# Local attention layers: a cell's attention in one piece instead of two halves, and a new order of the cell's steps

## The chip, the core and the metric

The kernel runs on one core of a Trainium2 chip. The core has five engines with queues of their own, each of which takes its instructions strictly in the order written: PE (TensorE: matrix products and transposes), DVE (VectorE), ACT (ScalarE: activations and copies), POOL (GpSimd) and SP (SyncE, which here issues every DMA). They meet only at semaphores. The metric is the time of one execution on the device in microseconds; the runs of a kernel are summed up by their median. The kernel before took 2453.49 us (median of three runs, 2446.65 to 2457.55).

## The reference

The program has two stages. The first (AdaLN, a 16-head attention, a mixture of experts, a linear-memory attention) is not touched by the change. The second is a stack of six local-attention layers, each followed by a gated feed-forward part, on four sequences (B) of 512 tokens with 128 channels:

```python
def attn_layer(x, Wqkv, qs, ksc, Wo):
    q, k, v = jnp.split(x @ Wqkv, 3, -1)          # 16 heads of 64
    q = l2norm(q) * qs
    k = l2norm(k) * ksc
    q = q * cos * scale + rotate_half(q) * sin * scale
    k = k * cos * inv + rotate_half(k) * sin * inv
    out = local_attention(q, k, v)                # windows of 32, each sees 64 keys
    return out @ Wo
...
for i in range(DEPTH):                            # 6 layers
    x = attn_layer(shift_tokens(x), ...) + x
    x = ffn_layer(shift_tokens(x), ...) + x
```

`local_attention` forms scores of 32 queries with 64 keys, masks them, takes a softmax over the 64 and multiplies with the values. `shift_tokens` moves half of the channels by one token.

## The kernel before

**Cells.** The work of the six layers is cut into 96 cells, numbered n: layer l, sequence b, group j of four heads (j = 0 to 3, the fastest). A cell's work is spread over four passes of one loop (`for n in range(-4, NC + 1)`). While cell n is in its attention, cell n+1 has its rotated queries and keys scaled and regrouped, cell n+2 gets its norms and values, and cell n+3 (`nx`) its projections.

**Steps and engines**, by line of the kernel before:

- `project(nx, w)`: two products into the PSUM tile `pq` (one buffer of two banks), w = 0 for queries, 1 for keys (L831).
- `rotate(nx, w)`: two DVE passes over `pq` (L841, L842), then two on POOL (L843, L844).
- `square(nx, w)`: ACT squares `pq` (L849). `pq` is free for the next projection after both.
- `norms(n+2)`: products into the bank `nb` (L859), a DVE clamp into `rn` (L868), Ln and Exp on ACT (L870, L872, each with a table load ahead of it), four DMAs into `rb` (L878). It calls `place("N")`, `place("L")`, `place("X")` between them.
- `scale(n+1)`: POOL multiplies keys and queries by `rb` (L886). `gather(n+1, w)`: four DMAs each into `kd` (keys) and `qd` (queries) (L899).
- `values(n+2)`: products into two banks (L910), each copied by ACT (L917), and three DMAs (L919 to L921).
- `scores(n, u)`: for half u of the windows, two mask products (L934), 64 small products (L940), DVE maximum and subtraction (L949, L951). `exponential` on ACT (L960), `normalise` on DVE (L965 to L967).
- `turn(n, u)`: four transposes (L974), a copy by ACT (L976). `weigh(n, u)`: 64 products with the values (L989), two copies (L1001).
- `output(n-1)`, in cells with even j: eight PE passes (L1009), added to `zT` by DVE (L1010).

**Feed-forward.** After the fourth group of a sequence `feed` runs as a coroutine: `place(name)` lets it go on where it has stopped at that name. Its stops are, in order: Z (two DMAs that shift `zT` into `xsf`, L809 and L810), D (mean `lm`, L1037; subtraction L1039; square L1041), N (variance `lv`, L1044), L (Ln, L1046), X (Exp, L1048), A (normalised input `xn`, L1051 and L1052), B (two hidden products `phf`, L1022), G (gelu, L1027), B (two more), G, C (gate, L1031), A (two more with gates), B (result `pyf`, L1072). It spans four cells: Z and D fall into the cell with j = 0, N to G into j = 1, B and G into j = 2, C, A, B into j = 3.

**What sets the order.** Nothing reorders: each engine's queue is the order in which the loop calls the steps. The pool `ps_g` holds two banks for `nb`, the values, `output` and all products of `feed`.

Of the kernel before, what the change touches and what calls it, by code (L numbers as in the profile page):

```python
# [46 lines left out]
def adaln_kernel(ctx: ExitStack, tc: tile.TileContext, a: dict):  # L47
# [368 lines left out]
    class First:  # L416
# [41 lines left out]
        def settle(self):  # L458
            pass
# [307 lines left out]
    with ExitStack() as ph:  # L767
# [83 lines left out]
        def norms(n):  # L851

            d = live[n]
            nb = bank("nb", (P, S // 2))
            for h in range(2):
                for w in range(2):
                    for x in range(2):
                        c = 32 * (2 * w + x)
                        mm(  # L859
                            nb[c : c + 32, :],  # L860
                            nsel,
                            d["sq", w][:, h, x * (S // 2) : (x + 1) * (S // 2)],
                            start=(h == 0),
                            stop=(h == 1),
                            skip_group_check=True,
                        )
            rn = att.tile([P, S // 2], F32, name="rn")
            vec.tensor_scalar(rn, nb, 1e-24, None, ALU.max)  # L868
            place("N")
            act(rn, rn, AF.Ln, scale=65536.0)  # L870
            place("L")
            act(rn, rn, AF.Exp, scale=-0.5, bias=nsh_t)  # L872
            place("X")
            rb = d["rb"] = work.tile([P, 2, S], F32, name="rb", bufs=1)
            for w in range(2):
                for x in range(2):
                    c = 32 * (2 * w + x)
                    nc.sync.dma_start(  # L878
                        rb[:, w, x * (S // 2) : (x + 1) * (S // 2)],
                        rn[c : c + 32, :].unsqueeze(1).broadcast_to([32, 4, S // 2]),  # L880
                    )
# [6 lines left out]
        def gather(n, w):  # L888

            d = live[n]  # L890
            t = d["k" if w else "q"]
            if w:
                d["k"] = kts[n % 2]
                y = d["k"][:, :, WIN:]
            else:
                y = d["q"] = cel.tile([P, 2, S], F32, name="qd", bufs=2)
            for c in range(2):
                for h in range(2):
                    nc.sync.dma_start(y[h::2, c, :], t[64 * c : 64 * c + 64, h, :])  # L899

        def values(n):


            l, b, j = cells[n]
            c0 = 2 * INNER + j * 4 * HDW
            vo, ve = live[n]["v"] = vos[n % 3], ves[n % 3]
            for y in range(0, TB, 2):
                pv = bank("pv2", (P, 2, 4 * HDW))
                for t in range(2):
                    mm(  # L910
                        pv[:, t, :],
                        shifted[b][:, (y + t) * P : (y + t + 1) * P],
                        layers[l][0][:, c0 : c0 + 4 * HDW],
                        start=True,
                        stop=True,
                    )
                nc.scalar.copy(vo[:, y : y + 2, :], pv)  # L917
                yield
            nc.sync.dma_start(ve[0:64], vo[32:96])  # L919
            nc.sync.dma_start(ve[96:P], vo[0:32])  # L920
            nc.sync.dma_start(ve[64:96, 1:], vo[96:P, 0 : TB - 1])  # L921


        def scores(n, u):
            d = live[n]
            q, k = d["q"], d["k"]


            if u == 0:
                d["s"] = ps_s.tile([P, 2, UW, GK], F32, name="s2")  # L930
            s = d["s"][:, :, 4 * u : 4 * u + 4, :]
            for w in range(2):
                m = wmask_b[:, 1 if u == 0 and w == 1 else 0, 0:4, :]
                mm(s[:, w], ident_b, m, start=True, stop=False, skip_group_check=True)  # L934
            for i in range(4):
                for w in range(2):
                    t0 = (u * UW + 2 * i + (w + i + 1) % 2) * WIN
                    for x in range(4):
                        r, c = slice(64 * (x % 2), 64 * (x % 2) + 64), 32 * ((x + w) % 4)
                        mm(  # L940
# [4 lines left out]
                            stop=True,  # L945
                            skip_group_check=True,
                        )
            nm = att.tile([P, 2, 4], F32, name="nm2")
            vec.reduce_max(nm, s, axis=AX.X)  # L949
            p = d["p", u] = att.tile([P, UW, GK], F32, name="p2")  # L950
            vec.tensor_tensor(  # L951
                p.rearrange("p (i w) k -> p w i k", w=2),
                s,
                nm.unsqueeze(3).broadcast_to([P, 2, 4, GK]),
                ALU.subtract,
            )

        def exponential(n, u):
            p = live[n]["p", u]
            act(p, p, AF.Exp)  # L960

        def normalise(n, u):
            p = live[n]["p", u]
            sm = att.tile([P, UW], F32, name="sm2")
            vec.reduce_sum(sm, p, axis=AX.X)  # L965
            vec.reciprocal(sm, sm)
            vec.tensor_tensor(p, p, sm.unsqueeze(2).broadcast_to([P, UW, GK]), ALU.mult)  # L967

        def turn(n, u):

            p = live[n].pop(("p", u))
            pt = ps_t.tile([P, 4, P], F32, name="pt2", tag="pt2")
            for i in range(4):
                tr(pt[:, i, :], p[:, 2 * i : 2 * i + 2, :].rearrange("p w k -> p (w k)"), ident)  # L974
            pT = live[n]["pT", u] = att.tile([P, 4, P], F32, name="pT2")
            nc.scalar.copy(pT, pt)  # L976

        def weigh(n, u):
            d = live[n]
            pT = d.pop(("pT", u))  # L980

            po = [ps_o.tile([P, 2, 4, WIN], F32, name="po2"), ps_t.tile([P, 2, 4, WIN], F32, name="po2b", tag="pt2")]
            for i in range(4):
                for x in range(4):
                    c = 64 * (x % 2)
                    for w in range(2):
                        r = slice(64 * w, 64 * w + 64)
                        c1 = 32 * ((x + w) % 4)
                        mm(  # L989
                            po[w][c : c + 64, x // 2, i, :],  # L990
                            d["v"][(w + i) % 2][r, 2 * u + i // 2, 64 * x : 64 * x + 64],
                            pT[r, i, c1 : c1 + 32],
                            start=True,
                            stop=True,
                        )
            if u == 0:
                d["o"] = cel.tile([P, 2, 2, S // 2], F32, name="oT2", bufs=2)
            o = d["o"][:, u].rearrange("p h (a w q) -> p (h a) w q", w=4, q=WIN)
            for w in range(2):
                y = po[w].rearrange("p h (a b) q -> p (h a) b q", b=2)  # L1000
                nc.scalar.copy(o[:, :, 0::3, :] if w else o[:, :, 1:3, :], y)  # L1001

        def output(n):
# [76 lines left out]
        def place(name):  # L1080
# [3 lines left out]
            if running and running[1] == name:  # L1084
                try:
                    running[1] = next(running[0])
                except StopIteration:
                    running.clear()
                return True
            return False  # L1090

        turns = [(2, 3, 0, 0), (3, 0, 0, 1), (3, 1, 1, 0), (3, 2, 1, 1)]
        load_rotations(0)
# [2 lines left out]
        for n in range(-4, NC + 1):  # L1096
            nx = n + 3 if 0 <= n + 3 < NC else None
            here = 0 <= n < NC
            if here:
                scores(n, 0)  # L1100
            if 0 <= n + 1 < NC:
                scale(n + 1)
                gather(n + 1, 1)
            if n > 0:
                weigh(n - 1, 1)
            if here:
                exponential(n, 0)
            if 0 <= n + 2 < NC:
                norms(n + 2)
            elif n + 2 >= NC:  # L1110
                for name in "NLX":
                    place(name)
            place("C")
            if 0 <= n + 1 < NC:
                gather(n + 1, 0)
            if nx is not None:
                l, b, j = cells[nx]
                if l + 1 < DEPTH:
                    if (b, j) == (2, 0):
                        layers[l + 1] = load_layer(l + 1)  # L1120
                    if (b, j) == (2, 1):
                        load_rotations(l + 1)
                project(nx, 0)
            if here:
                normalise(n, 0)
            if nx is not None:
                rotate(nx, 0)
            if n > 0 and cells[n - 1][2] % 2 == 1:
                output(n - 1)
            place("Z")  # L1130
            if n + 4 < NC and cells[n + 4][2] == 0:
                b = cells[n + 4][1]
                shifted[b] = shift_in(b, xss[b % 2])
            if here:
                scores(n, 1)


            pieces = values(n + 2) if 0 <= n + 2 < NC else iter(())
            if n % 2:
                next(pieces, None)  # L1140
            if nx is not None:
                square(nx, 0)
            for _ in pieces:
                pass
            if here:
                exponential(n, 1)
            place("A")
            if here:
                turn(n, 0)
                normalise(n, 1)  # L1150
            if nx is not None:
                project(nx, 1)
                rotate(nx, 1)
            if here:
                weigh(n, 0)
            place("B")
            early_square = not place("G") and nx is not None
            if early_square:
                square(nx, 1)
            if here:  # L1160
                turn(n, 1)
            if nx is not None:
                if not early_square:
                    square(nx, 1)
                l, b, j = cells[nx]
                for b1, j1, w, h in turns:
                    if (b1, j1) == (b, j) and l + 1 < DEPTH:
# [109 lines left out]
```

## Time and profile before

| | us |
|---|---|
| median of three runs | 2453.49 |
| the profiled execution | 2440.67 |
| its span | 2438.9 |
| first mask product of the layers (L934) | 686.4 |
| first mask product of the last cell | 2388.2 |
| PE busy | 2164.8 (89%) |
| DVE / ACT / POOL busy | 1573.1 / 1400.7 / 1069.5 |

The layers thus take from about 686 us to the end. The 95 distances between the first mask products of neighbouring cells sum to 1701.8 us, 17.9 us a cell. In a layer's first two sequences the usual distances are 16.9 (j = 0), 16.2 (1), 18.0 (2) and 18.8 us (3), 69.9 us for a round of four. In the last two, when the next layer's weights and tables are loaded, single cells take 20 to 27 us. A page of the profile gives busy time by engine, the granted PE clock in 40 slices, and groups of instructions; a busy PE includes the time in which a product drains while the next is already running.

### The profile page before, as it was taken

What the parts mean: (1) busy time and instruction counts of PE and PEld (TensorE: products, weight loads), DVE (VectorE), ACT (ScalarE), POOL (GpSimd) and SP (SyncE); (2) the same over time, 40 slices, a digit from 0 to 9 for tenths busy, and PEclk for the clock granted to TensorE, in tenths of its full rate; (3) what the DMA queues carried; (4) which work ended last, traced back from release to release, by engine and by line L of the source; (5) the groups of instructions that cost most, each with busy time, mean ns of one, the idle gap of its engine ahead of it and who ended that gap; (6) DMA issues with size and microseconds to landing.
All of it is one profiled execution on the core that took longest, in us unless ns stands there. A gap on an engine that the chain in (4) does not pass through costs nothing.

```text
span 2438.9 us, 76498 instructions
## 1 busy us (share of the span) xinstructions
PE 2164.8 (89%) x33628; PEld 1233.3 (51%) x33628; DVE 1573.1 (65%) x2258; ACT 1400.7 (57%) x2211; POOL 1069.5 (44%) x690
## 2 busy tenths in 40 slices
PE   6889999887678998998899998999899998999996
PEld 3345454443245555555555555555555555555553
DVE  3344544443267677777677777777777777777873
ACT  1334334533356576666676766667666666676662
POOL 1000101010365475555755566555665556555550
PEclk9989999998799899999999999999999999999997
DMA  2200000000156745566555755557555665555550
GB/s 75 65 2 1 3 1 2 1 1 1 47 128 144 182 105 135 123 164 160 126 119 132 197 129 123 124 135 192 128 121 128 157 170 123 122 129 130 137 134 24
DMA packets 164760, 251.23 MB, mean 103 GB/s; under 512 B 28742, under 2 KB 90380, under 8 KB 163404
## 3 DMA queue, kind: packets, MB, share of 16 engines
q1 hardware_dynamic: 164428, 246.34, 41.7%
q8 instruction: 264, 4.33, 0.8%
q14 instruction: 68, 0.56, 0.1%
HBM read 34.27 MB, written 1.05 MB: 14 GB/s over the span
## 4 chain that ended last, share of the span: by engine, by line
PE 52%; DVE 11%; ACT 11%; issue 10%; SPq 5%; DMA 5%; POOL 5%; POOLq 0%; DVEq 0%; ACTq 0%
PE pq L831 7%; PE po L989 5%; PE py L1009 4%; PE s L286 4%; PE pv L910 4%; PE s L940 3%; DVE ur L842 3%; PE phf L1022 3%; PE pyf L1072 3%; PE ye L360 2%; PE nb L859 2%; DVE qr L841 2%; SPq L899 2%; PE p L342 2%; ACT sq L849 2%
## 5 line engine op out<-in xcount | busy, mean ns | idle before, releaser
L831 PE MATMUL pq<-xs,wqkv 128*128 128x512 f32 x768 | 383.7, 623 | 31.3 <-ACT sq L849 25.2
L843 POOL TENSOR_TENSOR kr<-kr,ur 128x512 f32<-128x512 f32 x96 | 122.1, 1272 | 453.8 <-DVE ur L842 402.7
L849 ACT ACTIVATE sq<-pq 128x1024 f32<-128x1024 f32 x192 | 197.4, 1028 | 187.2 <-DVE ur L842 180.9
L843 POOL TENSOR_TENSOR qr<-qr,ur 128x512 f32<-128x512 f32 x96 | 124.4, 1296 | 259.8 <-DVE ur L842 258.5
L967 DVE TENSOR_TENSOR p<-p,sm 128x512 f32<-128x512 f32 x192 | 230.6, 1201 | 6.6
L842 DVE TENSOR_TENSOR ur<-pq,tabs 128x1024 f32<-128x1024 f32 x192 | 232.7, 1212 | 0.0
L886 POOL TENSOR_TENSOR kr<-kr,rb 128x1024 f32<-128x1024 f32 x96 | 229.3, 2388 | 5.8 <-DMA rb<-rn 5.8
L886 POOL TENSOR_TENSOR qr<-qr,rb 128x1024 f32<-128x1024 f32 x96 | 231.0, 2406 | 0.0
L1001 ACT COPY oT<-po 128x256 f32<-128x256 f32 x192 | 71.6, 373 | 274.7 <-PE po2b L989 271.2
L831 PEld LDWEIGHTS pq<-xs,wqkv 128*128 128x128 f32 x768 | 136.7, 196 | 180.8 <-issue 147.0
L404 ACT ACTIVATE p<-s 128x1024 f32<-128x1024 f32 (+3 forms) x160 | 104.0, 701 | 189.1 <-PE s L286 149.2
L173 POOL TENSOR_TENSOR ln_rs<-ln_rs,mhalf 128x4 f32<-128x4 f32 x16 | 16.8, 1050 | 437.4 <-DVE ln_rs L172 437.4
L949 DVE TENSOR_REDUCE nm<-s 128x8 f32<-128x512 f32 x192 | 131.8, 687 | 111.9 <-PE s L940 111.9
L910 PE MATMUL pv<-wqkv,xs 128*128 128x256 f32 x768 | 198.5, 399 | 3.8 <-DVE zT L1010 2.9
L965 DVE TENSOR_REDUCE sm<-p 128x8 f32<-128x512 f32 x192 | 130.7, 681 | 102.8 <-ACT p L960 102.8
L940 PE MATMUL s<-kd,qd 64*32 64x64 f32 x12288 | 172.5, 227 | 24.2 <-DMA qd<-qr 20.2
L1022 PE MATMUL phf<-l_xc,w 128*128 128x512 f32 (+1 forms) x288 | 155.5, 654 | 40.7 <-ACT vo L917 36.6
L989 PE MATMUL po<-pT,vo 64*64 64x32 f32 x3072 | 164.3, 224 | 19.2 <-ACT pT L976 17.8
L989 PEld LDWEIGHTS po<-pT,vo 64*64 64x64 f32 x3072 | 126.7, 137 | 101.8 <-ACT pT L976 77.5
L940 PEld LDWEIGHTS s<-kd,qd 64*32 64x32 f32 x12288 | 138.8, 107 | 68.5 <-issue 47.7
L1009 PE MATMUL py<-oT,wo 128*128 128x512 f32 x384 | 172.8, 593 | 0.0
L989 PE MATMUL po2b<-pT,vo 64*64 64x32 f32 x3072 | 161.9, 222 | 4.7 <-issue 4.6
(198 smaller groups left out, 4896.2 us busy)
## 6 DMA issues: line engine op xcount, KB each, us to landing
rb<-rn SPq DMA_DIRECT2D x384, 128.0 KB
kd<-kr SPq DMA_DIRECT2D x384, 128.0 KB
qd<-qr SPq DMA_DIRECT2D x384, 128.0 KB
ve<-vo SPq DMA_DIRECT2D x96, 256.0 KB
tabs<-in_rope_dram SPq DMA_DIRECT2D x12, 1024.0 KB
ve<-vo SPq DMA_DIRECT2D x96, 128.0 KB
wqkv<-in_Wqkv_dram SPq DMA_DIRECT2D x6, 1536.0 KB
ve<-vo SPq DMA_DIRECT2D x96, 96.0 KB
```

The lines of the kernel that those rows point to most:

```text
L831: mm(pq[:, h, :], layers[l][0][:, c0 : c0 + P], shifted[b], start=True, stop=True)
L842: vec.tensor_tensor(u, d["pq"], t[:, 2 * w + 1], ALU.mult)
L843: pool_e.tensor_tensor(r[:, 0, :], r[:, 0, :], u[:, 1, :], ALU.subtract)
L849: act(d["sq", w], d.pop("pq"), AF.Square)
L886: pool_e.tensor_tensor(t, t, d["rb"][:, w, :].unsqueeze(1).broadcast_to([P, 2, S]), ALU.mult)
L910: mm(pv[:, t, :], shifted[b][:, (y + t) * P : (y + t + 1) * P], layers[l][0][:, c0 : c0 + 4 * HDW], start=True, stop=True,)
L940: mm(s[c : c + 32, w, i, :], q[r, x // 2, t0 : t0 + WIN], k[r, x // 2, t0 : t0 + GK], start=False, stop=True, skip_group_check=True,)
L949: vec.reduce_max(nm, s, axis=AX.X)
L967: vec.tensor_tensor(p, p, sm.unsqueeze(2).broadcast_to([P, UW, GK]), ALU.mult)
L989: mm(po[w][c : c + 64, x // 2, i, :], d["v"][(w + i) % 2][r, 2 * u + i // 2, 64 * x : 64 * x + 64], pT[r, i, c1 : c1 + 32], start=True, st ...
L1009: mm(py, layers[l][1][:, 2 * j - 2 + y, :], o[:, :, y % 2, :], start=(y == 0), stop=(y == 3))
L1022: mm(t[0:m], w1[:, w * DI + r0 : w * DI + r0 + m], xn, start=True, stop=True)
```

## The change

The attention of a cell is done for all 16 windows at once. Masks, maximum, subtraction, exponential and normalisation run on twice as many columns in half as many instructions; the scores and the products with values come in one run of 128. `scores` is split into `scores` (PE) and `settle` (DVE); `norms` is split into `norms` (up to the clamp, with N) and `invert` (Ln, Exp, the DMAs into `rb`, with L and X). The order in the loop is new:

```diff
+            if nx is not None:
...
+                        layers[l + 1] = load_layer(l + 1)
+                    if (b, j) == (2, 1):
+                        load_rotations(l + 1)
+            if here:
+                scores(n)
+            if 0 <= n + 1 < NC:
+                scale(n + 1)
+                gather(n + 1, 1)
+                gather(n + 1, 0)
+            if nx is not None:
                 project(nx, 0)
             if here:
-                normalise(n, 0)
+                settle(n)
+                exponential(n)
             if nx is not None:
                 rotate(nx, 0)
+            if n > 0:
+                weigh(n - 1)
+            if 0 <= n + 2 < NC:
+                norms(n + 2)
+            if nx is not None:
+                square(nx, 0)
+            if here:
+                normalise(n)
+            if 0 <= n + 2 < NC:
+                values(n + 2)
+                invert(n + 2)
...
+            place("C")
+            if nx is not None:
+                project(nx, 1)
+                rotate(nx, 1)
             if n > 0 and cells[n - 1][2] % 2 == 1:
                 output(n - 1)
             place("Z")
             if n + 4 < NC and cells[n + 4][2] == 0:
                 b = cells[n + 4][1]
                 shifted[b] = shift_in(b, xss[b % 2])
...
+                square(nx, 1)
             place("A")
             if here:
-                turn(n, 0)
-                normalise(n, 1)
...
+                turn(n)
+            place("B")
+            place("G")
...
             place("D")
```

The tiles `qd`, `p` and `pT` have one buffer instead of two. The new `turn` and `weigh` share two banks, one of each of the pools `ps_o` and `ps_t`:

```diff
+            pT = live[n]["pT"] = att.tile([P, UW, P], F32, name="pT2", bufs=1)
+            for u in range(2):
+                pt = (ps_o, ps_t)[u].tile([P, 4, P], F32, name="pt2", tag="pt2")
+                for i in range(4):
+                    g = 4 * u + i
+                    tr(pt[:, i, :], p[:, 2 * g : 2 * g + 2, :].rearrange("p w k -> p (w k)"), ident)
+                nc.scalar.copy(pT[:, 4 * u : 4 * u + 4], pt)
...
+            po = [(ps_o, ps_t)[w].tile([P, 2, 2, 4, WIN], F32, name=f"po{w}", tag="pt2") for w in range(2)]
```

PE's queue in a cell is before: scores (half 0), weigh of n-1 (half 1), norms, queries' projection, output, scores (half 1), values, turn (half 0), keys' projection, weigh (half 0), B, turn (half 1), D. It is after: scores, queries' projection, weigh of n-1, norms, values, keys' projection, output, turn, B, D. In the built program the two banks of `ps_g` go to whichever was released first: in cells with j = 1 (where `lv` still waits for its Ln) and j = 3 (where a hidden product waits for its gate) both pairs of value products use the bank of `nb`, one after the other.

More of the change, by code (lines that the diff above doesn't have):

```diff
@@ L866, in norms, with invert @@
                         )
-            rn = att.tile([P, S // 2], F32, name="rn")
+            rn = d["rn"] = att.tile([P, S // 2], F32, name="rn")
             vec.tensor_scalar(rn, nb, 1e-24, None, ALU.max)
             place("N")
+        def invert(n):
+            d = live[n]
+            rn = d.pop("rn")
             act(rn, rn, AF.Ln, scale=65536.0)
@@ L895, in gather @@
             else:
-                y = d["q"] = cel.tile([P, 2, S], F32, name="qd", bufs=2)
+                y = d["q"] = cel.tile([P, 2, S], F32, name="qd", bufs=1)
             for c in range(2):
@@ L917, in values @@
                 nc.scalar.copy(vo[:, y : y + 2, :], pv)
-                yield
             nc.sync.dma_start(ve[0:64], vo[32:96])
@@ L921, in values, with scores @@
             nc.sync.dma_start(ve[64:96, 1:], vo[96:P, 0 : TB - 1])
-        def scores(n, u):
+        def scores(n):
             d = live[n]
             q, k = d["q"], d["k"]
-            if u == 0:
-                d["s"] = ps_s.tile([P, 2, UW, GK], F32, name="s2")
-            s = d["s"][:, :, 4 * u : 4 * u + 4, :]
+            s = d["s"] = ps_s.tile([P, 2, UW, GK], F32, name="s2")
             for w in range(2):
-                m = wmask_b[:, 1 if u == 0 and w == 1 else 0, 0:4, :]
-                mm(s[:, w], ident_b, m, start=True, stop=False, skip_group_check=True)
-            for i in range(4):
+                mm(s[:, w], ident_b, wmask_b[:, w], start=True, stop=False, skip_group_check=True)
+            for i in range(UW):
                 for w in range(2):
-                    t0 = (u * UW + 2 * i + (w + i + 1) % 2) * WIN
+                    t0 = (2 * i + (w + i + 1) % 2) * WIN
                     for x in range(4):
@@ L947, in scores, with settle @@
                         )
-            nm = att.tile([P, 2, 4], F32, name="nm2")
+        def settle(n):
+            d = live[n]
+            s = d.pop("s")
+            nm = att.tile([P, 2, UW], F32, name="nm2")
             vec.reduce_max(nm, s, axis=AX.X)
-            p = d["p", u] = att.tile([P, UW, GK], F32, name="p2")
+            p = d["p"] = att.tile([P, 2 * UW, GK], F32, name="p2", bufs=1)
             vec.tensor_tensor(
@@ L953, in scores, with exponential, normalise, turn @@
                 s,
-                nm.unsqueeze(3).broadcast_to([P, 2, 4, GK]),
+                nm.unsqueeze(3).broadcast_to([P, 2, UW, GK]),
                 ALU.subtract,
             )
-        def exponential(n, u):
-            p = live[n]["p", u]
+        def exponential(n):
+            p = live[n]["p"]
             act(p, p, AF.Exp)
-        def normalise(n, u):
-            p = live[n]["p", u]
-            sm = att.tile([P, UW], F32, name="sm2")
+        def normalise(n):
+            p = live[n]["p"]
+            sm = att.tile([P, 2 * UW], F32, name="sm2")
             vec.reduce_sum(sm, p, axis=AX.X)
             vec.reciprocal(sm, sm)
[L967 to L978, printed above, removed]
+            vec.tensor_tensor(p, p, sm.unsqueeze(2).broadcast_to([P, 2 * UW, GK]), ALU.mult)
+        def turn(n):
+            p = live[n].pop("p")
+            pT = live[n]["pT"] = att.tile([P, UW, P], F32, name="pT2", bufs=1)
[5 more added lines that the diff above has]
+                nc.scalar.copy(pT[:, 4 * u : 4 * u + 4], pt)
+        def weigh(n):
             d = live[n]
-            pT = d.pop(("pT", u))
-            po = [ps_o.tile([P, 2, 4, WIN], F32, name="po2"), ps_t.tile([P, 2, 4, WIN], F32, name="po2b", tag="pt2")]
-            for i in range(4):
+            pT = d.pop("pT")
+            po = [(ps_o, ps_t)[w].tile([P, 2, 2, 4, WIN], F32, name=f"po{w}", tag="pt2") for w in range(2)]
+            for i in range(UW):
                 for x in range(4):
@@ L989, in weigh @@
                         mm(
-                            po[w][c : c + 64, x // 2, i, :],
-                            d["v"][(w + i) % 2][r, 2 * u + i // 2, 64 * x : 64 * x + 64],
+                            po[w][c : c + 64, i // 4, x // 2, i % 4, :],
+                            d["v"][(w + i) % 2][r, i // 2, 64 * x : 64 * x + 64],
                             pT[r, i, c1 : c1 + 32],
@@ L995, in weigh @@
                         )
-            if u == 0:
-                d["o"] = cel.tile([P, 2, 2, S // 2], F32, name="oT2", bufs=2)
-            o = d["o"][:, u].rearrange("p h (a w q) -> p (h a) w q", w=4, q=WIN)
+            d["o"] = cel.tile([P, 2, 2, S // 2], F32, name="oT2", bufs=2)
+            o = d["o"].rearrange("p u h (a w q) -> p (u h a) w q", w=4, q=WIN)
             for w in range(2):
-                y = po[w].rearrange("p h (a b) q -> p (h a) b q", b=2)
+                y = po[w].rearrange("p u h (a b) q -> p (u h a) b q", b=2)
                 nc.scalar.copy(o[:, :, 0::3, :] if w else o[:, :, 1:3, :], y)
@@ L1088, in place @@
                     running.clear()
-                return True
-            return False
         turns = [(2, 3, 0, 0), (3, 0, 0, 1), (3, 1, 1, 0), (3, 2, 1, 1)]
@@ L1098, in adaln_kernel @@
             here = 0 <= n < NC
[L1099 to L1115, printed above, removed]
             if nx is not None:
@@ L1122, in adaln_kernel @@
                         load_rotations(l + 1)
+            if here:
[5 more added lines that the diff above has]
+            if nx is not None:
                 project(nx, 0)
             if here:
-                normalise(n, 0)
+                settle(n)
+                exponential(n)
             if nx is not None:
                 rotate(nx, 0)
+            if n > 0:
[9 more added lines that the diff above has]
+                invert(n + 2)
+            elif n + 2 >= NC:
+                for name in "NLX":
+                    place(name)
+            place("C")
+            if nx is not None:
+                project(nx, 1)
+                rotate(nx, 1)
             if n > 0 and cells[n - 1][2] % 2 == 1:
@@ L1133, in adaln_kernel @@
                 shifted[b] = shift_in(b, xss[b % 2])
[L1134 to L1140, printed above, removed]
-            if nx is not None:
[L1142 to L1146, printed above, removed]
+            if nx is not None:
+                square(nx, 1)
             place("A")
             if here:
-                turn(n, 0)
-                normalise(n, 1)
+                turn(n)
+            place("B")
+            place("G")
             if nx is not None:
[L1152 to L1164, printed above, removed]
                 l, b, j = cells[nx]
```

## The prediction

> **What bounds the kernel now.** I read the page first (busy time, then PE and clock in slices), then the waits of PE, then the timeline of one round of four cells, engine by engine.
>
> ```profile
> PE 2164.8 (89%) x33628; PEld 1233.3 (51%) x33628; DVE 1573.1 (65%) x2258; ACT 1400.7 (57%) x2211; POOL 1069.5 (44%) x690
> ...
> PEclk9989999998799899999999999999999999999997
> ```
>
> PE is the bound, nearly always at full clock. How much is work and how much waiting? From the timeline I take, for each group of products, the shortest distance from its start to the start of the next group (from 860 us on): masks 0.31 and scores 0.79 (a half), projection 1.81, weigh 1.06 (a half), norms 1.00, values 1.83, turn 0.44 (a half), output 3.43, `lm` 0.86, `lv` 0.96, two hidden products 1.78, `pyf` 2.68. A cell's attention is 2 x 1.10 + 2 x 1.81 + 2 x 1.06 + 1.00 + 1.83 + 2 x 0.44 = 11.65 us; a round of four cells 4 x 11.65 + 2 x 3.43 + 0.86 + 0.96 + 3 x 1.78 + 2.68 = 63.3. Quiet rounds take 69.9, so PE waits only 6.6 us in a round, in small pieces:
>
> ```profile
> PE phf L1022 <- ACT vo L917: 36.6, 36, 1.8
> ...
> PE pq L831 <- ACT sq L849: 25.2, 28, 3.7
> ...
> PE pt L974 <- ACT oT L1001: 20.3, 27, 0.8
> ...
> PE s L940 <- DMA qd<-qr: 20.2, 20, 2.3
> ```
>
> (Total us, times, longest.) What any new order must keep hidden are two long chains of `feed`. The first ends in `lm`: `output`, the add to `zT`, two DMAs into `xsf`, mean.
>
> ```profile
> 1633.72 2.56 SPq L878 DMA_DIRECT2D rb<-rn  x4
> 1636.32 3.13 SPq L899 DMA_DIRECT2D qd<-qr  x4
> 1639.85 0.46 SPq L809 DMA_DIRECT2D xsf<-zT  x1
> 1640.36 0.60 SPq L810 DMA_DIRECT2D xsf<-zT  x1
> ...
> 1642.89 1.10 PE L1037 MATMUL lm<-xsf,mean_w 128*128 128x512 f32 x2
> ```
>
> `output` ended at 1635.2, and 1.10 + 1.83 + 0.44 + 1.81 + 1.06 + 0.44 = 6.7 us of PE work stand between it and `lm`; even so `lm` starts just when `xsf` has landed, 1.9 us after its second DMA was issued. The second chain goes from `lv` over ACT's Ln and Exp to `xn` and the hidden products:
>
> ```profile
> 1647.30 1.28 ACT L870 ACT_TABLE_LOAD   x1
> 1648.84 0.42 ACT L870 ACTIVATE rn<-rn 128x256 f32<-128x256 f32 x1 [0.25 <-DVE rn L868]
> 1649.43 0.69 ACT L1046 ACTIVATE ge<-lv,eps_t 128x512 f32<-128x512 f32 x1 [0.18 <-PE lv L1044]
> 1650.14 1.28 ACT L872 ACT_TABLE_LOAD   x1
> 1651.43 0.51 ACT L872 ACTIVATE rn<-rn,nsh_t 128x256 f32<-128x256 f32 x1
> 1651.85 0.61 ACT L1048 ACTIVATE ge<-ge 128x512 f32<-128x512 f32 x1
> ```
>
> Ln stands early on ACT's queue, ahead of the copies of values. That is what moves.
>
> **What the merge saves.** Masks twice as wide: half as many with twice the columns, 0.31 becomes 0.52; 128 scores in a run 1.42 (9.85 ns each, 0.16 once); 128 products with values 1.97 (14.2 ns each, 0.15 once). Saved: 2.20 - 1.94 + 2.12 - 1.97 = 0.41 us a cell (11.65 becomes 11.24), 1.6 a round, 39 us in 24 rounds. All of it is on PE. DVE and ACT lose fixed parts too (a maximum of 1024 columns, taken as 1.22 like the 1212 ns of L842, for 2 x 0.69; an Exp of 1.06 for 2 x 0.64), worth nothing while they have slack. The single buffers cost nothing: `qd` is written from the end of POOL's scaling, at least 5 us into a cell, and its scores are over at 2.0; `p` and `pT` are read a whole step before they are written again.
>
> **The cell laid out anew.** Time from the first mask; durations from the rows; 0.05 us from engine to engine. PE: scores to 1.94, queries' projection to 3.76, weigh to 5.73, norms to 6.73. DVE: maximum and subtraction 2.0 to 4.46, the two rotations to 6.83, `rn` to 7.3. ACT: Exp to 5.5, weigh's two copies (0.59 each, behind weigh) 5.8 to 7.0, square 8.05. First values 7.64, second 8.56 (behind `rn`), the keys' projection, free of `pq` since 8.05, to 10.37. ACT: copies of values to 9.4, table load 1.28, Ln 0.42, table load 1.28, Exp 0.51: **12.95**, against Exp at 1633.7 in a cell begun at 1626.7, 7.0, before. `normalise` is done by 11 even when POOL slows its last multiplication (L967, 1201 ns in the mean for 512 columns, 690 alone); turn comes later. POOL works 4.8 + 5.1 us of a cell, its scaling starts when `rb` has landed, about 1 us into the next cell, and `qd` lands near 10, 6 us before its scores. So:
>
> - **j = 2**: no wait; 11.24 + 3.43 + 1.78 = 16.5 (18.0 before).
> - **j = 3**: the second hidden product holds a bank until its gate, now after values. First values wait for `rn` (0.6), second for the first's copy (0.9), `pyf` for the second gate (0.6): 11.24 + 1.78 + 2.68 + 2.1 = 17.8 (18.8).
> - **j = 0**: SP's queue now has `rb` ahead of `xsf`: 12.95 + 2.56 = 15.5, two issues to 16.7, landed 18.6. On PE only turn is left after `output`: 14.7. PE sits **4.0 us** before `lm`; 11.24 + 3.43 + 0.86 + 4.0 = 19.5 (16.9).
> - **j = 1**: `lv` to 7.7, first values 8.6, their copy 9.4, second values (wait 0.9), copy 11.25; table load, Ln 12.95, Ln of `lv` 13.65, table load, Exp 15.45, Exp 16.1, `xn` 0.68 + 0.9 (0.55 with POOL idle, 1.34 in the mean): 17.65. Turn ends at 13.1. PE sits **4.55 us** before the hidden products; 11.24 + 0.96 + 1.78 + 0.9 + 4.55 = 19.4 (16.2).
>
> A round: 73.2 against 69.9, +3.3; in 24 rounds +79 us. Once these stalls stand, square, copies and gathers have time: nothing else is late behind them.
>
> **Two rules.** In the trace a gap does more than its length:
>
> ```profile
> 922.50:925.90 3.40, 1.00 (x5) 0.71 (x6) 1.82 (x2) 2.13 (x4) 1.50 (x2) 1.00 0.61 141
> 925.91:929.32 3.41, 3.41 (x92) 1.80 (x90) 1.13 (x2) 0.63 (x1) 3.41 (x3) 0.51 0.57 156
> ```
>
> (Window, its length, busy PE, PEld, DVE, ACT, POOL, then the granted clock.) 3.4 us with PE busy for 1.00, then 3.41 us at half clock. The sixteen drops between 870 and 2340 us all follow gaps of 0.9 to 4.2 us, most of 1.7 to 2.3, in windows 0 to 0.54 busy. The Trainium skill (TensorE: Matmul & The Clock Gate, The HAM clock gate) speaks of an idle window of about 3.4 us, free-running. By the rule, gaps of 4.0 and 4.55 hold a whole window in (4.0 - 3.41)/3.41 = 17% and 33% of the rounds: half a drop a round. By the trace, each gap makes one. A drop costs up to 1.7 us; I take 1.3, since part of it lies in the gap. Trace: 2.6 x 24 = 62 us, less some 21 for drops of before that go: +41. Rule: 16 less 21, nothing. I take the trace.
>
> The same skill (ScalarE: Activation LUTs, What ACT_TABLE_LOAD costs) gives 2.66 us a switch, 1283 ns and a drain of 1380. Their number is unchanged, but two now lie in each stalling chain. The ACT rows above follow the load without a drain: 1650.14 + 1.28 is 1651.43. By the rule each gap would be 2.8 us longer, +132 us; I take the rows.
>
> **Moved in queues.** `load_layer` and `load_rotations` now issue ahead of both gathers. Five layers; the seven loads took 5.8 us of SP at 1657 to 1663. The lower bound is nothing (the next scores in the j = 1 cell come at 19.4, `qd` issued at 12 lands near 15), the upper 6 x 5 = 30 us. I take nothing: `qd` already came last before.
>
> **Sum.** 2440.7 + 79 + 41 = 2561 for the profiled execution; the median of the runs stands 0.5% above it, so **2574**.
>
> **The rivals.**
> - Forecast, both gaps with half clock: 2574, 2520 to 2640 with loads and errors of 1 us a gap. Chance 0.57.
> - The gaps without the clock (mostly hidden in them): 2440.7 + 79 = 2520, as a median 2533. For: by the rule it should be rare. Against: the rows. 0.25.
> - **Not slower**: the two chains stay hidden, and PE's work decides. For: 39 us of PE work go, j = 2 and 3 gain 2.5 us a round, ACT and DVE have a third of their time free. It takes over from where `xsf` lands by 15 and `xn` is ready by 13.5, 4 us earlier in both; Exp at 12.95 would have to come at 9. Then 2440.7 - 39 = 2402, as a median 2414. 0.12.
> - The gaps half as long and no clock: +79 becomes near 0, 2453. 0.04.
> - Loads in front of gathers at their upper bound on top of the forecast: 2605. 0.02.
>
> No change, within 0.5% (12 us, about what this measurement can tell), 0.04; faster 0.12; slower 0.84. The range, 2470 to 2640, leaves out the faster case and what lies above.
>
> **What would show it.** PE idle before `lm` released by the `xsf` DMA, near 4 us in each of 24, and before the first hidden product, released by DVE; Exp of `rn` 13 us into a cell; cells of 19.5, 19.4, 16.5 and 17.8 us; some 40 drops of the clock; rows of 1.2 us for maximum and subtraction; PE busy at most 40 us below 2165 apart from half clock. I am wrong if cells with j = 0 and 1 don't lengthen.

## The result and the profile after

The changed kernel takes **2632.27 us** (median of four runs, 2623.97 to 2643.15) against 2450.37 us before (the three runs above and a fourth): 1.0732 times as long, with a 95% interval of 1.069 to 1.0774. The profiled execution took 2623.97 us, its span is 2622.1. The prediction was 2574 (2470 to 2640): the sign and the range held, but the time lies near the upper end of the range, 58 us above the middle forecast.

The page of the changed kernel, busy time and granted clock in 40 slices:

```profile
PE 2175.9 (83%) x33340; PEld 1231.8 (47%) x33436; DVE 1441.1 (55%) x1778; ACT 1385.9 (53%) x1923; POOL 1067.2 (41%) x690
...
PEclk8899999897899988999999998999989999989998
```

PE is busy for about as long as before (2175.9 us for 2164.8), DVE for 132 us less; the span has grown by 183 us. So work didn't come in; waiting did. Part of PE's work has also become slower: the mean granted clock fell from 0.956 to 0.92, and that hides a saving. At full clock the distance from the first mask to the queries' projection is 1.94 us and weigh takes 1.99, against 2 x 1.10 and 2 x 1.06 before: 0.39 us saved in each cell. (The 1.94 is from e6_loads, whose scores are the same; in the trace of the changed kernel the records of the first of the two mask products are missing, all 96, so that the same distance reads 1.72 there. Cells of this trace begin 0.2 us earlier than their first record.)

The waits of PE in the changed kernel (total us, times, longest):

```profile
PE phf L1027 <- DVE l_xc L1057: 119.1, 24, 5.8
...
PE lm L1042 <- DMA xsf<-zT: 98.8, 24, 4.9
...
PE pv L914 <- ACT vo L921: 30.4, 45, 0.7
```

Of the first two, the kernel before has this (its wait ahead of `lm`, and its first hidden products in a cell with j = 1, which follow the products with values without a wait):

```profile
PE lm L1037 <- DMA xsf<-zT: 13.9, 7, 3.7
...
1657.76 1.98 PE L1022 MATMUL phf<-l_xc,w 128*128 128x512 f32 x4
```

Now both come once in every round, 24 times: 119.1/24 = 5.0 us ahead of the first hidden products and 98.8/24 = 4.1 us ahead of `lm`. One round in the timeline, the first mask product recorded in its cell with j = 0 at 1322.4:

```profile
1335.64 2.56 SPq L882 DMA_DIRECT2D rb<-rn  x4
1338.30 0.55 SPq L809 DMA_DIRECT2D xsf<-zT  x1
1338.90 0.59 SPq L810 DMA_DIRECT2D xsf<-zT  x1
...
1336.05 1.04 PE L981 MATMUL pt<-ident,p 128*128 128x128 f32 x8
1341.37 1.18 PE L1042 MATMUL lm<-xsf,mean_w 128*128 128x512 f32 x2 [4.28 <-DMA xsf<-zT]
```

`rb` goes out first, then `xsf`; PE has done its last transposes at 1337.1 and waits until 1341.4. In the next cell, ACT, DVE and PE:

```profile
1354.81 1.28 ACT L874 ACT_TABLE_LOAD   x1
1356.11 0.42 ACT L874 ACTIVATE rn<-rn 128x256 f32<-128x256 f32 x1
1356.43 0.67 ACT L1051 ACTIVATE ge<-lv,eps_t 128x512 f32<-128x512 f32 x1
1357.12 1.28 ACT L876 ACT_TABLE_LOAD   x1
1358.41 0.51 ACT L876 ACTIVATE rn<-rn,nsh_t 128x256 f32<-128x256 f32 x1
1358.83 0.61 ACT L1053 ACTIVATE ge<-ge 128x512 f32<-128x512 f32 x1
...
1359.47 0.70 DVE L1056 TENSOR_TENSOR l_xc<-l_xc,ge 128x512 f32<-128x512 f32 x1 [1.19 <-ACT ge L1053]
1360.21 1.37 DVE L1057 TENSOR_SCALAR l_xc<-l_xc,prm 128x512 f32<-128x512 f32 x1
...
1361.73 3.75 PE L1027 MATMUL phf<-l_xc,w 128*128 128x512 f32 x4 [4.96 <-DVE l_xc L1057]
```

The same two table loads and activations as before, abutting, but each link waits only for the one above it, and PE has nothing left to do. And the four hidden passes take 3.75 us where they took 1.98. The windows around both gaps (PE busy is the third column, the granted clock the last but two):

```profile
1338.85:1342.26 3.41, 0.90 (x2) 0.40 (x3) 0.00 (x0) 0.00 (x0) 1.51 (x1) 1.00 0.82 212
1342.26:1345.67 3.41, 3.19 (x131) 2.32 (x131) 0.94 (x2) 0.63 (x1) 3.15 (x2) 0.50 0.40 85
1355.92:1359.33 3.41, 0.84 (x8) 0.60 (x6) 2.36 (x2) 3.37 (x6) 0.97 (x1) 1.00 0.52 144
1359.33:1362.74 3.41, 1.01 (x2) 0.53 (x3) 2.07 (x2) 3.27 (x5) 1.97 (x2) 0.50 0.62 135
1362.74:1366.15 3.41, 3.19 (x5) 0.95 (x4) 0.00 (x0) 1.32 (x2) 2.23 (x1) 0.50 0.07 21
1366.15:1369.50 3.35, 3.35 (x133) 2.02 (x132) 1.55 (x2) 1.34 (x2) 2.44 (x2) 1.00 0.56 118
```

A window in which PE was busy for 0.8 to 1.0 us is followed by one at half clock. The gap before the hidden products spoils two windows, so half clock lasts 6.8 us and covers all four passes.

The cells, as distances of first mask products, means over all rounds, with the time at half clock in a round of the layers (from the clock records of the trace, from 840 us on). Where records of first mask products are missing, a cell's start is taken from the second; single cells are certain to about 0.2 us, rounds better:

| kernel | j = 0 | 1 | 2 | 3 | round | half clock | span |
|---|---|---|---|---|---|---|---|
| before | 17.7 | 15.9 | 18.4 | 19.8 | 71.7 | 2.8 | 2438.9 |
| changed | 21.0 | 23.5 | 17.0 | 17.9 | 79.4 | 11.7 | 2622.1 |

Cells with j = 2 and 3 did become shorter, by 3.3 us together. Those with 0 and 1 lost 10.9. The next layer's weights are loaded in the second sequence of a layer (from its cell with j = 1 on, where cell n+3 is already one of the third); its rounds are the long ones, 83.5 us in the mean here.

### The profile page after: what moved, and what is told of

The parts are those of the page before. It is cut to its first block, busy times and chain, and to the rows that moved or that the text cites. A ratio compares the mean times of both kernels' runs of the same rounds, so it can differ in the third digit from the quotient of the medians.

```text
span 2622.1 us, 75717 instructions
## 1 busy us (share of the span) xinstructions
PE 2175.9 (83%) x33340; PEld 1231.8 (47%) x33436; DVE 1441.1 (55%) x1778; ACT 1385.9 (53%) x1923; POOL 1067.2 (41%) x690
## 4 chain that ended last, share of the span: by engine, by line
PE 64%; ACT 11%; DVE 8%; issue 6%; SPq 5%; DMA 4%; POOL 2%; ACTq 0%; POOLq 0%; DVEq 0%
PE pq L831 9%; PE po L995 7%; PE pv L914 7%; PE s L940 5%; PE phf L1027 5%; PE s L286 4%; PE nb L859 3%; PE py L1014 3%; SPq L882 3%; ACT L874 2%; ACT L876 2%; DMA xsf<-zT 2%; PE ye L360 2%; PE pyf L1077 2%; PE p L342 2%
## 5 line engine op out<-in xcount | busy, mean ns | idle before, releaser
L831 PE MATMUL pq<-xs,wqkv 128*128 128x512 f32 x768 | 383.8, 623 | 19.5 <-ACT sq L849 11.7
L953 DVE TENSOR_REDUCE nm<-s 128x16 f32<-128x1024 f32 x96 | 117.6, 1225 | 310.4 <-PE s L940 310.4
L964 ACT ACTIVATE p<-p 128x1024 f32<-128x1024 f32 x96 | 101.6, 1058 | 349.6 <-DVE p L955 349.6
L1027 PE MATMUL phf<-l_xc,w 128*128 128x512 f32 (+1 forms) x288 | 181.2, 763 | 122.7 <-DVE l_xc L1057 119.1
L995 PEld LDWEIGHTS po<-pT,vo 64*64 64x64 f32 x6144 | 196.3, 137 | 81.1 <-issue 80.7
L995 PE MATMUL po<-pT,vo 64*64 64x32 f32 x6144 | 209.2, 222 | 10.5 <-issue 10.1
L995 PE MATMUL po<-pT,ve 64*64 64x32 f32 x6144 | 206.9, 222 | 6.8 <-issue 6.8
L831 PEld LDWEIGHTS pq<-xs,wqkv 128*128 128x128 f32 x768 | 142.4, 196 | 135.4 <-issue 107.5
L995 PEld LDWEIGHTS po<-pT,ve 64*64 64x64 f32 x6144 | 194.0, 137 | 10.8 <-issue 10.5
L914 PEld LDWEIGHTS pv<-wqkv,xs 128*128 128x128 f32 x768 | 137.0, 191 | 122.2 <-ACT vo L921 48.7
L921 ACT COPY vo<-pv 128x512 f32<-128x512 f32 x192 | 112.4, 586 | 114.7 <-PE pv L914 113.0
```

What stands on the lines that cost most here:

```text
L831: mm(pq[:, h, :], layers[l][0][:, c0 : c0 + P], shifted[b], start=True, stop=True)
L914: mm(pv[:, t, :], shifted[b][:, (y + t) * P : (y + t + 1) * P], layers[l][0][:, c0 : c0 + 4 * HDW], start=True, stop=True,)
L995: mm(po[w][c : c + 64, i // 4, x // 2, i % 4, :], d["v"][(w + i) % 2][r, i // 2, 64 * x : 64 * x + 64], pT[r, i, c1 : c1 + 32], start=True ...
L1027: mm(t[0:m], w1[:, w * DI + r0 : w * DI + r0 + m], xn, start=True, stop=True)
```

## The experiments

All are edits of the changed kernel; where one builds on an earlier one, that is said. The table of results comes first; its ratios are to runs of the kernel before made next to each experiment, whose medians lie between 2453.56 and 2454.34 us.

| run | what | j = 0 | 1 | 2 | 3 | half clock | span | ratio to before (95%) |
|---|---|---|---|---|---|---|---|---|
| e1_fill | PE kept busy in both gaps | 20.2 | 21.5 | 17.2 | 18.0 | 1.6 | 2557.6 | 1.0403 (1.0316 to 1.049) |
| e7_fill_lm | in the gap before `lm` alone | 20.3 | 22.8 | 17.1 | 17.8 | 6.8 | 2591.0 | 1.0611 (1.0521 to 1.0701) |
| e10_half_fill | half of each gap | 20.4 | 22.1 | 17.3 | 17.9 | 4.4 | 2585.0 | 1.0566 (1.0504 to 1.0627) |
| e2_lm | `lm` later | 15.3 | 28.4 | 17.3 | 17.9 | 11.5 | 2620.5 | 1.0618 (1.0514 to 1.0723) |
| e8_lm_xs | e2 and `xs` early | 15.2 | 24.6 | 17.3 | 17.8 | 7.4 | 2510.1 | 1.0252 (1.0176 to 1.0328) |
| e3_hidden | hidden products later | 20.9 | 15.0 | 21.2 | 18.2 | 7.1 | 2529.3 | 1.031 (1.0224 to 1.0397) |
| e6_loads | loads behind gathers | 20.8 | 22.8 | 16.7 | 18.8 | 13.1 | 2615.5 | 1.0646 (1.0591 to 1.0701) |
| e4_both | e2 and e3, `lv` later | 14.9 | 20.0 | 21.3 | 18.1 | 9.5 | 2506.6 | 1.0254 (1.0187 to 1.0321) |
| e5_best | e4 and three moves | 15.3 | 15.3 | 22.1 | 18.7 | 4.4 | 2442.1 | 0.9908 (0.9877 to 0.994) |
| e9_best2 | e5 and two moves | 15.2 | 13.8 | 20.1 | 19.3 | 2.1 | 2373.9 | 0.9643 (0.9608 to 0.9678) |

### Is the second half of the loss the clock? (e1, e7, e10)

```diff
+        def busy(k):
+            t = ps_s.tile([P, 2, UW, GK], F32, name="s2")
+            for i in range(k):
+                mm(t[:, i % 2], ident_b, wmask_b[:, 0], start=True, stop=True)
...
             yield "D"
+            busy(17)
             pm = bank("lm")
...
+            busy(20)
             t0, t1 = hidden(1, 0), hidden(1, 1)
```

> The changed kernel with 17 products of 128 x 512 in bf16 ahead of lm and 20 ahead of the first hidden products (3.6 and 4.3 us at full clock), whose results nobody reads. Clock theory: the changed kernel lost 79.4 - 73.2 = 6 us a round to half clock after the two gaps; with PE kept busy the drops go (half clock in a round from 11.7 to under 3 us), cells with j = 0 and 1 take about 19.6 each, a round 73 to 74 us, the span 2480 to 2510 (from 2622). Rival (the chains themselves are longer than laid out, the clock only follows): rounds stay above 78, the span above 2590.

Half clock went from 11.7 to 1.6 us a round, and the span fell by 64.5 us with 37 products that nobody reads added to each round. So the clock is a cause, not a sign. But only half of what I expected came back: the span stayed at 2557.6, above 2510. What is left of the two waits in e1:

```profile
PE phf L1032 <- DVE l_xc L1063: 16.1, 23, 1.5
...
PE lm L1048 <- DMA xsf<-zT: 11.5, 23, 1.2
```

PE still waits at the end of both, so the filling itself delays nothing. The hidden products wait 0.7 us each behind 4.26 us of filling: with the clock up, these products still start 18.7 us into the cell (median), where the layout said 17.65. The chain itself is longer than laid out.

e7 keeps the filling before `lm` (17 products) and drops the other.

> The changed kernel with the 17 products of e1 ahead of lm alone, none ahead of the hidden products. Clock theory: of the 64 us that e1 gained over the changed kernel the gap before lm has the larger part, since its half clock falls on the scores and the products with values at the head of j = 1: j = 0 near 20.0, j = 1 from 23.3 to about 21.3, the span 2570 to 2585. Rival (both gaps share it, or the hidden products have it): j = 1 stays above 22.3, the span above 2595.

The span fell by 31 us, half of what e1 gained, between the two expectations. j = 1 typically took 21.9 us (20.4 in e1, 22.9 unfilled). Each gap has about one half of the clock's loss (30 of 75 us by the medians of the runs, which differ among themselves by up to 20 us); that the one before `lm` has the larger part is not borne out.

e10 leaves a part of each gap idle: `busy(8)` and `busy(12)` in the same places.

> The changed kernel with 8 products nobody reads ahead of lm and 12 ahead of the first hidden products, so that PE's unbroken idle time is near 2.3 us in both gaps (from 4.1 and 5.0), well under the 3.4 us of a window. If the clock falls only after a wholly idle window, it must stay up as in e1: half clock under 2 us a round, the span near 2557. If a window less than half busy is enough, as the trace of before shows, a drop follows two gaps in three: 5 to 7 us of half clock a round, the span 2580 to 2605.

The waits of PE in e10:

```profile
PE lm L1048 <- DMA xsf<-zT: 58.9, 24, 3.6
PE phf L1032 <- DVE l_xc L1063: 55.6, 23, 3.3
```

The gaps are 2.4 us each, shorter than a window, and still the clock falls. One window of 3.41 us with such a gap, and the next:

```profile
1724.55:1727.96 3.41, 1.04 (x4) 0.40 (x3) 0.00 (x0) 0.00 (x0) 1.46 (x1) 1.00 0.96 247
1727.96:1731.38 3.42, 3.42 (x132) 1.96 (x129) 0.69 (x1) 0.63 (x1) 3.21 (x2) 0.50 0.89 327
```

From 840 us on there are 44 such gaps and 27 drops; 21 of the drops follow one of the gaps, about one in two rather than two in three (the other six follow stops within the products with values, see the last section). The span lies in the interval given for "less than half busy" and the time at half clock, 4.4 us a round, a little under it. So an unbroken idle window isn't needed. Taken over all windows of that stretch, the 22 in e10 and the 13 in the kernel before in which PE was busy for less than 0.4 were all followed by half clock; between 0.4 and 0.5 it was 3 of 15 and 4 of 7, and above 0.6 two of some 450 and none of 430. The limit thus lies a little under one half, in these two traces.

### Do the two gaps come from the order? (e2, e8, e3)

```diff
                 exponential(n)
+            place("D")
             if nx is not None:
                 rotate(nx, 0)
...
-            place("D")
```

> The changed kernel with the stop D (lm and its subtraction and square) moved from the end of the cell into the next cell, behind the queries' projection. Gap theory: lm no longer waits, cells with j = 0 fall from 20.9 to about 15, those with j = 1 from 23.2 to about 20.5 (0.9 for lm, less some 3 of half clock that followed the gap), a round from 79.4 to about 71, the span about 2420. Rival (the wait only moves on, to lv, which now follows sooner behind the square): lv waits 2 us or more, a round stays above 75, the span above 2510.

The wait for `xsf` is gone, j = 0 fell to 15.3 as expected, and the time hardly moved (span 2620.5 after 2622.1): j = 1 rose to 28.4. Not `lv` waits, though, but something I had not seen behind the gap. PE's waits in e2:

```profile
PE phf L1027 <- DVE l_xc L1057: 119.4, 24, 5.8
PE pq L831 <- DMA xs<-zT: 81.2, 20, 5.6
```

81.2/20 = 4.1 us: the next sequence's first projection waits for `xs`, whose DMAs are issued right behind those of `xsf`. The gap before `lm` had covered it. e8 issues them at the head of that cell (`zT` of that sequence has long been final):

```diff
+            if n + 4 < NC and cells[n + 4][2] == 0:
+                b = cells[n + 4][1]
+                shifted[b] = shift_in(b, xss[b % 2])
             if here:
                 scores(n)
```

> The kernel of e2 with the two DMAs into xs at the head of the cell with j = 0. Theory (e2 didn't gain because the next sequence's projection then waited for xs, which stood behind rb and xsf on SP's queue): that wait of 3.9 us goes, j = 0 stays at 14.7, j = 1 falls from 28.5 to 21 or 22 with the gap before the hidden products still there, a round about 72, the span 2420 to 2460. Rival (the projection then waits for something else): j = 1 above 25, the span above 2530.

The wait for `xs` is gone, and the span is 110 us lower than in e2. It is still 50 us above the interval given, and the round stays at 74.9 rather than 72:

```profile
PE phf L1027 <- DVE l_xc L1057: 119.1, 24, 5.8
PE lm L1042 <- DMA xsf<-zT: 37.3, 24, 3.8
```

`lm` in its new place still waits 1.6 us for `xsf` in the mean, and j = 1 keeps the gap before the hidden products, 5.0 us, with its half clock.

e3 attacks that gap alone: `feed` stops at a new name H after X, does A, B and G a cell later (j = 2), and the second hidden pair at a new place E, behind the queries' projection of j = 3. C is called ahead of `norms`, A ahead of `output`.

```diff
             act(sq, sq, AF.Exp, scale=-0.5)
+            yield "H"
             yield "A"
...
-            yield "B"
+            yield "E"
             t0, t1 = hidden(1, 2), hidden(0, 2)
-            yield "G"
             gelu(2, t0)
```

> The changed kernel with the first hidden products moved a cell later, from the end of j = 1 to the end of j = 2, and the second pair to just behind the queries' projection of j = 3; the gate moved ahead of norms. lm stays as changed. Gap theory: cells with j = 1 fall from 23.2 to about 16.3 (still slowed by the half clock behind lm), j = 2 stays at 16.6, j = 3 about 18.2, a round about 72, the span about 2450. Rival (the gap moves with the products): j = 2 gains what j = 1 loses and a round stays above 76, the span above 2540.

j = 1 fell to 15.0, further than expected; j = 2 rose from 17.0 to 21.2, so part of the gap did move with the products. In j = 2 the queries' projection starts 1.9 us later than without a wait (3.59 us after the recorded mask, in place of 1.72): in a short j = 1 cell the late square (behind Ln and Exp on ACT) has not yet freed `pq`. The hidden products then wait 2.2 us behind the transposes (medians). Net 93 us of span, about half of what was expected.

### Are the loads in front of the gathers a cost? (e6)

The loads go back behind the two gathers:

```diff
-            if nx is not None:
-                l, b, j = cells[nx]
...
             if here:
                 scores(n)
             if 0 <= n + 1 < NC:
                 scale(n + 1)
                 gather(n + 1, 1)
                 gather(n + 1, 0)
+            if nx is not None:
+                l, b, j = cells[nx]
...
                 project(nx, 0)
```

> The changed kernel with the loads of the next layer issued behind the gathers again, as before the change; nothing else. Queue theory: the loads in front of the gathers cost 3 to 5 us in each cell with j = 1 of the second sequence (26 us against 23) and 1 to 2 in the next, some 24 us in five layers: the time falls by 15 to 30 us. Rival (it is the traffic of the loads, wherever they are issued): those cells stay above 25 us or others lengthen as much, the time moves by less than 8 us.

Unclear. The medians differ by 20 us (2612 against 2632), but the intervals of the two ratios just overlap. In the profiled executions the five cells with j = 1 of the second sequence fell from 26.2 to 22.8 us in the mean, and the five with j = 3 after them rose from 18.1 to 21.9: so the cost of the loads moved rather than vanished, and the spans differ by only 7 us.

### Is there a version without the gaps? (e4, e5, e9)

e4 is e2 and e3 together, with N taken out of `norms` and placed behind the keys' projection.

> Both moves together, and lv moved behind the keys' projection so that the second values don't wait for a bank. Theory: nothing but PE's own work is left, 61.7 us a round, with about 2 us where the projection of the next cell waits for the late square of j = 1: rounds of 63 to 67 us, the span 2260 to 2350, faster than the kernel before by 4 to 7%. Rival (another limit takes over: rb, POOL's scaling and the gathers in cells of 14 us, or the loads of the layers): rounds near 70, the span 2400 or more.

```profile
PE pq L831 <- DMA xs<-zT: 90.2, 21, 6.3
PE phf L1026 <- ACT pT L981: 51.7, 22, 3.0
PE pq L831 <- ACT sq L849: 37.9, 25, 3.7
```

A miss: 2506.6, not 2350. All three waits of e2 and e3 that stood behind the gaps are here: `xs`, `xn` in j = 2, and the late square. (The profile names the copies of `pT` for the second, but the hidden products don't read `pT`; in the cell with j = 2 begun at 1316.0 they start 0.15 us after `xn` is ready, as they do in e1. `xn` stands there on DVE behind a multiplication of 2.69 us (1.22 at the shortest in the changed kernel) and the two passes of a rotation.) e5 takes the first away, puts N between values and the keys' projection, and puts the loads back:

```diff
+            if n + 4 < NC and cells[n + 4][2] == 0:
+                b = cells[n + 4][1]
+                shifted[b] = shift_in(b, xss[b % 2])
             if here:
                 scores(n)
...
                 values(n + 2)
+            place("N")
             if nx is not None:
                 project(nx, 1)
-            place("N")
```

> The kernel of e4 with three moves more: the two DMAs that shift the next sequence into xs go to the head of the cell with j = 0 (in e4 the next projection waited 4 us for them), lv goes between values and the keys' projection, and the loads of the next layer go back behind the gathers. Theory (each wait seen so far is one of order, none of throughput): j = 1 falls from 20 to about 13.5, j = 2 from 21 to 18 or 19 (its projection still waits about 1 us for the late square), a round 64 to 69 us, the span 2290 to 2380, faster than the kernel before by 2.5 to 6%. Rival (in a cell of 13 us the chain Exp, rb, POOL's scaling, rotations becomes the bound): rounds above 71, the span above 2420.

0.9908: less than 1% faster than the kernel before, not 2.5 to 6%. j = 1 came down to 15; j = 2 did not, with 3.4 us of wait in the mean before its hidden products:

```profile
PE phf L1026 <- ACT pT L981: 70.9, 21, 7.8
```

e9 computes `xn` where DVE is idle anyway, at the head of j = 2 while the scores run, and moves D behind `weigh`:

```diff
             yield "H"
-            yield "A"
             xn = xc
...
                 weigh(n - 1)
+            place("D")
             place("C")
```

> The kernel of e5 with xn computed at the head of the cell with j = 2, while DVE waits for the scores (in e5 it stood behind both rotations, and the hidden products waited 3.2 us), and D one step later, behind the products with values (lm waited 1.2 us for xsf). Theory: j = 2 falls from 21 to about 18, j = 1 from 14.9 to about 14, a round from 70.3 to 66 or 67, the span from 2442 to 2350 to 2370, 3 to 4.5% faster than the kernel before. Rival (POOL, still late in j = 2 since rb lands 5 us into it, holds the rotations and with them the next projection): j = 2 stays above 20, the span above 2410.

The page of e9 and its waits:

```profile
PE 2119.9 (89%) x33340; PEld 1214.8 (51%) x33436; DVE 1476.9 (62%) x1778; ACT 1346.8 (57%) x1900; POOL 1091.7 (46%) x690
```

```profile
PE phf L1026 <- DVE zT L1014: 28.7, 5, 7.6
PE pq L831 <- ACT sq L849: 27.0, 23, 3.7
PE po L994 <- issue: 21.3, 18, 2.6
PE pyf L1075 <- DVE ge L1035: 17.7, 22, 2.9
```

2368.10 us in the median, 0.9643 of the time before (0.9608 to 0.9678): the attention in one piece, with `feed` placed so that its two chains lie under other work, beats both kernels. How much of its gain over the kernel before is the merge and how much the order is not shown: no run has the new order with the attention in halves. Rounds without loads take 65.4 us (medians), a little under what was expected. The span is 4 us above the interval given, and j = 2 takes 20.1 us in the mean (18.7 in rounds without loads), at the edge of what the rival said: ten cells of the second sequence, two for each layer loaded, take 23 to 28 us. There the rival is right in part. Five times PE waits up to 7.6 us for a bank, since DVE is late, DVE waits for POOL, and POOL for `rb`. In one of them (selected lines of SP, ACT and POOL):

```profile
1069.53 0.59 SPq L59 DMA_DIRECT2D wqkv<-in_Wqkv_dram  x1
...
1071.86 0.51 ACT L875 ACTIVATE rn<-rn,nsh_t 128x256 f32<-128x256 f32 x1
...
1081.09 2.57 SPq L881 DMA_DIRECT2D rb<-rn  x4
...
1085.89 2.35 POOL L889 TENSOR_TENSOR kr<-kr,rb 128x1024 f32<-128x1024 f32 x1 [10.12 <-DMA rb<-rn]
```

`rn` is ready at 1072.4, but `rb` is issued 8.7 us later, since the loads and the DMAs into `ve` stand ahead of it on SP's queue. In all five load rounds of e9 this lag is 8.2 to 9.2 us; in the changed kernel, where the loads stand ahead of the gathers, it is nothing. So the place of the loads matters after all once the cells are short; no run here moves them behind `rb`.

## Why the prediction was right, and where its size was off

**The mechanism held at each step.** PE waits before `lm` for the `xsf` DMA, 4.1 us (4.0 predicted), and before the first hidden products for DVE, 5.0 us (4.55), 24 times each. Exp of `rn` ends 13.0 us into the cell shown (12.95), and two small waits that the layout had are there, 0.7 us for the copy of the first values (0.9) and 0.5 for the second gate (0.6). Cells with j = 2 and 3 take 17.0 and 17.9 us (16.5 and 17.8). e3 and e8 take one gap each away, and e9 both: the span falls by 93, 112 and 248 us. So the order of the steps is what made the kernel slower, and not the merged attention, which saves 0.39 us a cell (0.41 predicted).

**Row against rule, twice.** The row was right on the clock. The rule of the Trainium skill (TensorE: Matmul & The Clock Gate, The HAM clock gate), a drop after a wholly idle window, would have given half a drop a round; there are two, and in e10 drops follow gaps of 2.4 us, well short of a window. The row was right on the table loads too: in the changed kernel Ln starts 0.02 us after its load, as before, and the drain of 1380 ns that the skill gives (ScalarE: Activation LUTs, What ACT_TABLE_LOAD costs) does not show.

**What was mis-sized is above all the cell with j = 1.** In rounds without loads (medians over the first, third and fourth sequences) the cells take 21.0, 22.9, 16.9 and 17.9 us, 78.7 in all; the sum of the prediction, with its 1.3 us of half clock for each gap, had 20.8, 20.7, 16.5 and 17.8, 75.8 in all. That is 2.9 us a round, some 70 us in 24 rounds: all of the difference between the 2561 us of the sum and the 2624 of the profiled execution. Against e1 (19.9, 20.4, 16.4, 17.9 in such rounds, 74.6) it falls into two about equal terms:

- *The clock*, 78.7 - 74.6 = 4.1 us a round, taken as 2.6. I had priced a drop as one window, "up to 1.7 us"; 26 of the 48 drops lasted two. In 19 of these 26 the first window at half clock was itself less than half busy (0.14 to 0.47); in the 22 drops of one window it was busy for 0.77 or more. So a gap of 4 to 5 us can spoil two windows. The half clock also fell where it hurts: on scores, weigh and norms at the head of j = 1, through which the second chain runs.
- *The chain*, 74.6 - 73.2 = 1.4 us a round, of which 1.0 in j = 1. Of that, half is the second step of `xn`: it takes 1.37 us in 22 of its 24 cases, in which POOL is at work on the rotations for most of it, and 0.55 in the two others. I had taken 0.9, between the two, though the kernel before has the same 22 cases. The rest is spread along the chain: in the cell of e1 begun at 1323.7 the last Exp ends 0.3 us later than laid out, and PE starts 0.15 us after `xn` is ready.

The credit of 21 us for drops of before that would go, and the excess of load rounds carried over unchanged, didn't hold one by one either (in the changed kernel the rounds of the last two sequences, 78.5 us, cost little more than those of the first, 77.0, and only the second's cost 83.5), but they nearly cancel: by the rounds (71.7 in the mean against 69.9 before, 79.4 against 78.7 after) the excess shrank by some 26 us.

**The rivals.** "Not slower" failed at the point it named: `xsf` landed at 19.1 in the cell shown, not by 15. The case without the clock didn't come, with two drops in every round; e1, which nearly takes them away, shows about what it would have been, a span of 2557.6 in place of 2520. That the range held is in part luck: the chain's extra length and the dearer drops both went the same way, and a little more would have left it. The moved loads, taken as nothing, stay open for the changed kernel (e6).

## What to carry to other kernels

When steps are merged or reordered in queues that run in order, find for each chain that crosses engines how much work of the bounding engine stood between its two ends, and lay the chain out again in the new order: here 6.7 us of cover became 0.9, and that decided the sign where 0.4 us of saved work in each cell could not. A long gap hides the waits behind it (`xs`, the late square), so a gap that is removed may give nothing back until the next wait goes too. A gap on TensorE is to be priced with the windows of its clock: here two of 4 to 5 us cost some 4 us more in a round without loads, and 2.7 in the mean over all rounds (64.5 us in 24, e1).

## What the hardware showed unexpectedly

The products of the layers, those with values above all, sometimes stop in the middle for 1 to 3 us with nothing to wait for in the profile ("issue", 21.3 us in 18 cases in e9), mostly in rounds with loads. One such case in the changed kernel:

```profile
1750.46 0.24 PE L995 MATMUL po<-pT,vo 64*64 64x32 f32 x1 [2.38 <-issue]
```

The DMA engines were 88 to 99% busy around it and moved 249 to 345 GB/s. The packet records of the traces say what PE waits for. A queue of its own brings instructions in packets of 16 KB (q8, "instruction" on the page); here one landed at 1749.1, 1.3 us before PE went on. In the twelve traces there are 144 such stops of more than 0.6 us in the layers, and 141 of them end 1.1 to 1.7 us after the end of such a packet, where only 7 to 8% of all moments lie. That is strong evidence, though of timing alone, that the instructions come late. Why their packets do is less sure: in the 4 us ahead of a stop the DMA engines are 96% busy in the median, against 53 to 62% over the layers, but no run changes that load alone.
